# An attention block with an FFN gate on one core: sums over x's quarters taken by token and turned on TensorE, the gate's product spread over the next block, statistics and a square root moved in the prologue

## The chip, the cores and the metric

The kernel runs on one core of a Trainium2 chip, in one launch. The metric is the device time of the launch in microseconds (us). The kernel before took 1982.35 us as the median of three runs (1981.34 to 1983.27).

The engines are named as in the profile: PE is TensorE (PEld its weight loads), DVE is VectorE, ACT is ScalarE, POOL is GpSimd, and SP is the engine from whose queue nearly all DMAs are issued. In the timeline every engine's instructions stand in the order in which the program lists them.

## The reference

The input x has 8 sequences of 256 tokens with 512 features, all in float32. It is normalized, and goes through an attention with 128 heads (latent and rotary parts, head size 4 + 64) and through an FFN whose output, after a SiLU, gates the attention's output:

```python
xn = _layernorm(x, axis=-1)
s = _L0_attn_ref(xn, ...)                    # 128 heads
def _qlora_linear(x, wq, A, B):
    w = jnp.tile(wq, (1, 4))                 # the weight is one quarter, repeated four times
    return x @ w.T + (x @ A.T @ B.T) * 0.5
gate = silu(_qlora_linear(xn, w1q, a1, b1)); up = _qlora_linear(xn, w3q, a3, b3)
g = silu(_qlora_linear(gate * up, w2q, a2, b2))   # hidden size 1376
return x + s * g
```

As each FFN weight is a quarter repeated four times, x @ w.T is the sum of x's four quarters (128 features each) times the quarter. The kernel forms that sum, called xs here, once per block of tokens, and does the same for the hidden layer (function fold).

## The kernel before, in words

**Two phases.** The first phase (function first_phase) computes the layernorm, the FFN's gate and the narrow projections, for the 2048 tokens in four blocks of 512 (index tb, 0 to 3), each of four tiles of 128 tokens (index n). The second phase does attention, block after block of heads; it starts with the score matmuls of L828, and the changed lines do not touch it.

**No scheduler.** The order of the work on each engine is the order in which the Python code writes it. The tile framework only places buffers and adds the waits. PSUM's eight banks of 128x512 float32 come from one pool (function bank). Other buffers rotate by tag: gate and gs and hT have two each, x tiles (xt) six.

**The prologue.** DMAs are issued on SP for x's first block, then the weights, then the six small rows of the LoRA factors (chunk_rows), then x's second block. PE runs 26 transposes of the identity (warm), and four matmuls that spread a weight row over all partitions (first, L627), whose results ACT copies (L635); then two more warm transposes. Function norm takes the statistics with DVE (BN stats and aggregate, L416 and L417, two instructions a tile), and forms 1/sqrt(variance + eps): a bit trick (L428, L430) and three Newton steps, for block 0 on DVE (L436 to L438) and for the other blocks on POOL (L440 to L443, then L449 and L450). Function norm_one applies it, for block 0 on DVE (L459), for others on ACT (L457). Function turn transposes x's tiles on PE (xpt, 16 transposes, L467) and copies them to SBUF as act, features on partitions.

**xs.** Function sums adds the four feature chunks of act: DVE L479, POOL L480 at the same time, DVE L481, and ACT copies the result (L482). xs exists twice, as its row 0 is replaced by a different LoRA row in each (L505). Functions less_first and rest_less_first take the replaced row's weights out of w1 and w3 (L643 on DVE, L655 on POOL).

**One block.** For tb the code calls main(tb, u) for u = 0 to 5. Each but the last makes two pairs of products px and py from xs and w1, w3 (four 128x512 results), then DVE adds the LoRA term (L541 into gate, L545 into hT or in place), ACT takes SiLU of gate (L544), and the product gate * up goes to POOL (L558) or DVE (L556, and L551 and L552 at u = 4 and 5). At u = 3 and 5 fold (POOL, L570 to L572) and low_out (pm2, L582) follow. The next block's x is prepared alongside: norm_one at the u given in the code, and turn at u = 4. After u = 5 come, in this order, sums, narrow (pm and the DVE operation mid, L497, whose rows go to DRAM and come back broadcast as low), low_out(tb, 2) with three DVE operations L594, down (pp, and POOL's differences of x, L158, written to DRAM), gate_out (pf, 48 matmuls, then SiLU into gs, L608, and a DMA to gates_d), and the statistics of block tb + 2. After block 0 POOL lays out weights for the attention (set_up, L744 to L756). In block 3 the first four Project units of the attention are computed among u = 2 to 5.

**Names of places.** on_columns (L173) issues the four matmuls that make one 128x512 result. load_x(tb + 2) is issued on SP at u = 1 and has to wait, for two of its tiles, until turn(tb + 1) has read the buffers.

Of the kernel before, what the change touches and what calls it, by code (L numbers as in the profile page):

```python
# [37 lines left out]
def mla_ffn_gate_kernel(  # L38
# [275 lines left out]
    def first_phase(between):  # L314
# [16 lines left out]
        def load_x(tb):  # L331
            xts[tb] = []
            for n in range(4):
                t = f1.tile([P, D], F32, tag="xt", name=f"xt_{tb}_{n}", bufs=6)
                nc.sync.dma_start(out=t, in_=x[ds(tb * TB + n * P, P), :])
                xts[tb].append(t)
# [22 lines left out]
        for k, wt in enumerate((w1t, w3t)):  # L359
            nc.scalar.dma_start(out=rows[65 + 32 * k : 66 + 32 * k], in_=wt[0:1, :])  # L360
        chunk_rows = f2.tile([P, TB], F32, tag="gs", name="chunk_rows")[:, 0:P]
# [29 lines left out]
        for w_sb, wt in ((w1_sb, w1t), (w3_sb, w3t)):  # L391
            load_chunks(nc.sync, w_sb, wt)

# [13 lines left out]
        load_x(1)  # L407
# [11 lines left out]
        def norm(tb):  # L419


            for n in range(4):
                norm_part(tb, n)
# [3 lines left out]
            i0 = f2.tile([P, 4], I32, tag="i0", name=f"i0_{tb}")  # L427
            nc.vector.tensor_single_scalar(i0, ve.bitcast(I32), 1, ALU.logical_shift_right)  # L428
            r0 = f2.tile([P, 4], I32, tag="r0", name=f"r0_{tb}")
            nc.vector.tensor_scalar(r0, i0, -1.0, float(0x5F3759DF), ALU.mult, ALU.add)  # L430
            r = r0.bitcast(F32)
            e = f2.tile([P, 4], F32, tag="e", name=f"e_{tb}")
            for step in range(3):
# [26 lines left out]

        def turn(tb):
# [12 lines left out]
        def sums(tb):  # L474

            a = xnT[tb]
            xs = [f1.tile([P, TB], F32, tag=f"xs{k}", name=f"xs{k}_{tb}") for k in range(2)]
            xs2 = f1.tile([P, TB], F32, tag="tmp", name=f"xs2_{tb}")
            nc.vector.tensor_add(xs[0], a[:, 0, :], a[:, 1, :])  # L479
            nc.gpsimd.tensor_add(xs2, a[:, 2, :], a[:, 3, :])  # L480
            nc.vector.tensor_add(xs[0], xs[0], xs2)  # L481
            nc.scalar.copy(xs[1], xs[0])  # L482
            xsum[tb] = xs
# [10 lines left out]
        def narrow(tb):  # L494
# [6 lines left out]
            for k in range(2):  # L501
                t = f1.tile([P, TB], F32, tag=f"low{k}", name=f"low{k}_{tb}")
                nc.sync.dma_start(out=t, in_=low_d[tb][k : k + 1, :].to_broadcast([P, TB]))
                lows[tb].append(t)
                nc.scalar.copy(xsum[tb][k][0:1], mid[32 * k : 32 * k + 1])  # L505
# [92 lines left out]
        def gate_out(tb):  # L598
            pfs = [bank(f"pf_{tb}_{n}") for n in range(4)]
            for ks in ((0, 1), (2,)):  # L600
                for n in range(4):
# [4 lines left out]
            for n in range(4):  # L606
# [24 lines left out]

        for i in range(2):
            for k in range(2):
                ps = bank(f"first_{k}_{i}").rearrange("p (q m) -> p q m", q=2)
                nc.scalar.copy(*spread_first(k, ps, *parts[k][i]))  # L635
        warm(2)
# [20 lines left out]
        stats = norm(0)  # L657
# [3 lines left out]
        sums(0)  # L661
        less_first(0, nc.gpsimd)
        narrow(0)
        less_first(1, nc.vector)
        between(-1)
# [7 lines left out]
        rest_less_first(1)  # L673
        for tb in range(NTB):
            more = tb + 1 < NTB
            for u in range(6):
                pj = None
# [10 lines left out]
                if u == 1 and tb == 0:  # L688
                    stats = norm(1)
                if more:  # L690
                    for n in range(4):
                        if u == (n if tb else 2 + n // 2):
                            norm_one(tb + 1, n, *stats)
                if u == 4 and more:
                    turn(tb + 1)
                if u == 1 and tb + 2 < NTB:
                    load_x(tb + 2)
# [6 lines left out]
            if more:  # L704
                sums(tb + 1)
# [5 lines left out]
            gate_out(tb)  # L711
            if tb == 0:
                between(0)
            if tb + 2 < NTB:
                stats = norm(tb + 2)
# [416 lines left out]
```

## Time and profile before

| what | value |
|---|---|
| median of three runs | 1982.35 us |
| the profiled execution's own time | 1983.69 us |
| its span, first to last instruction | 1981.9 us |
| mean granted TensorE clock | 0.998 |
| PE busy | 1964.4 us (99%) |
| DVE, ACT, POOL busy | 1575.9, 1098.0, 758.3 us |
| PE busy from 0 to 218.58 us (first phase) | 206.84 us |

The span is what the trace covers. Times within it count from its start. A timeline row gives an instruction's start and length, the engine, the line, the operation, its output and inputs, and in brackets the idle time of that engine before it and what ended that idle time. PEclk is the share of the full TensorE clock that was granted. An instruction's own length is a little more than the step from one to the next of its kind, since they overlap.

### The profile page before, as it was taken

To read this page: it belongs to the slowest core of one execution; us is meant where nothing else is said; L and a number is where in the kernel's file an instruction comes from. 1 tells how busy PE (TensorE), PEld (TensorE's weight loads), DVE (VectorE), ACT (ScalarE), POOL (GpSimd) and SP (SyncE) were. 2 spreads that over 40 slices of the span, in tenths; PEclk is the share of its full clock that TensorE was granted. 3 is DMA by queue.
4 is the path that set the end of the run, shared out by engine and by line. 5 is a ranking of instruction groups with operands and counts; after the bars stand their busy time and mean duration, and the time that the engine had idled before them with its cause. 6 is when DMAs were issued, how large, how long until landed. Compare 5 with 4: busy or idle time off the path is not lost.

```text
span 1981.9 us, 78697 instructions
## 1 busy us (share of the span) xinstructions
PE 1964.4 (99%) x34033; PEld 1309.7 (66%) x34033; DVE 1575.9 (80%) x2666; ACT 1098.0 (55%) x3029; POOL 758.3 (38%) x1113
## 2 busy tenths in 40 slices
PE   8999999999999999999999999999999999999998
PEld 4334567767777766667776766667776767676775
DVE  7764678888787877788787878788787878888888
ACT  3333465566556555566556555566556555655654
POOL 5877445544552323332332323322332323233232
PEclk9999999999999999999999999999999999999999
DMA  6235322222232223322232322321232222122212
GB/s 195 100 118 179 114 87 87 77 77 87 75 125 89 100 87 101 100 85 68 87 103 89 99 87 101 100 84 69 87 104 88 99 87 86 67 87 87 72 50 87
DMA packets 120017, 187.02 MB, mean 94 GB/s; under 512 B 10715, under 2 KB 84843, under 8 KB 119673
## 3 DMA queue, kind: packets, MB, share of 16 engines
q1 hardware_dynamic: 119665, 181.97, 27.3%
q8 instruction: 270, 4.42, 0.9%
q14 instruction: 74, 0.61, 0.1%
q10 hardware_dynamic: 8, 0.02, 0.0%
HBM read 147.86 MB, written 34.10 MB: 92 GB/s over the span
## 4 chain that ended last, share of the span: by engine, by line
PE 93%; POOL 2%; DVE 2%; issue 1%; DMA 1%; ACT 0%; SPq 0%; POOLq 0%; ACTq 0%; DVEq 0%
PE q L173 40%; PE sc L828 35%; PE av L879 11%; PE po L173 2%; PE pf L173 1%; PE py L173 1%; PE qq L249 1%; PE px L173 1%; POOL h4b L571 0%; POOL hT L558 0%; DVE ring L854 0%; POOL h L570 0%; PE pm L173 0%; DMA xt<-in_x_dram 0%; PE pp L173 0%
## 5 line engine op out<-in xcount | busy, mean ns | idle before, releaser
L847 ACT ACTIVATE pr<-sc,nmx 128x256 f32<-128x256 f32 x2048 | 814.6, 500 | 463.3 <-DVE nmx L841 459.1
L841 DVE TENSOR_REDUCE nmx<-sc 128x2 f32<-128x512 f32 x1024 | 635.5, 683 | 281.7 <-PE sc L828 257.4
L854 DVE STREAM_TRANSPOSE ring<-pr 128x512 f32<-128x512 f32 x1024 | 635.0, 678 | 0.0
L216 POOL TENSOR_TENSOR e<-e,e 128x256 f32<-128x256 f32 x128 | 93.8, 733 | 1042.5 <-ACT e L211 558.8
L173 PE MATMUL q<-x,ws 128*32 128x256 f32 x8192 | 489.0, 379 | 0.7 <-POOL ws L137 0.7
L828 PE MATMUL sc<-act,qr 32*128 32x256 f32 x8192 | 488.3, 374 | 0.0
L828 PEld LDWEIGHTS sc<-act,qr 32*128 32x128 f32 x8192 | 420.7, 185 | 21.8
L173 PEld LDWEIGHTS q<-x,ws 128*32 128x32 f32 x8192 | 266.6, 110 | 176.3 <-POOL ws L137 1.1
L173 PE MATMUL q<-x,w 128*32 128x256 f32 x6144 | 381.7, 381 | 0.9 <-DVE py L545 0.8
L173 PEld LDWEIGHTS q<-x,w 128*32 128x32 f32 x6144 | 187.4, 110 | 155.6 <-ACT pr L847 35.6
L828 PE MATMUL sc<-kc,qcm 32*128 32x256 f32 x4096 | 280.7, 387 | 0.0
L828 PEld LDWEIGHTS sc<-kc,qcm 32*128 32x128 f32 x4096 | 198.0, 184 | 65.0 <-issue 50.4
L879 PE MATMUL av<-ring,vpad 128*32 128x256 f32 (+1 forms) x4160 | 233.4, 376 | 0.1
L211 ACT COPY e<-q 128x256 f32<-128x256 f32 x512 | 202.4, 396 | 26.5 <-PE q L173 26.5
L900 ACT ACTIVATE acc<-av,sides_sb 128x128 f32<-128x128 f32 (+1 forms) x172 | 60.5, 420 | 244.6 <-PE av L879 244.6
L879 PEld LDWEIGHTS av<-ring,vpad 128*32 128x32 f32 x4160 | 134.6, 110 | 88.3 <-issue 1.6
L269 POOL TENSOR_TENSOR qcm<-qc,mask_sb 128x1024 f32<-128x1024 f32 x64 | 122.2, 1910 | 0.0
L217 POOL TENSOR_TENSOR e<-e,e 128x256 f32<-128x256 f32 x128 | 93.6, 731 | 10.0
L218 POOL TENSOR_TENSOR qr<-e,e 128x256 f32<-128x256 f32 x128 | 93.5, 731 | 10.0
L310 POOL COPY vpad<-vall 32x128 f32<-32x128 f32 x256 | 75.4, 294 | 10.2 <-PE av L879 2.3
L228 DVE TENSOR_TENSOR qr<-e,q 128x256 f32<-128x256 f32 x128 | 53.9, 421 | 23.0 <-POOL e L216 17.5
L541 DVE SCALAR_TENSOR_TENSOR gate<-low,bcol_sb,px 128x512 f32<-128x512 f32 x44 | 32.8, 745 | 45.0 <-POOL hT L558 25.7
(124 smaller groups left out, 1138.0 us busy)
## 6 DMA issues: line engine op xcount, KB each, us to landing
w<-in_w_rope_dram SPq DMA_DIRECT2D x128, 512.0 KB
ws<-sums_d SPq DMA_DIRECT2D x96, 512.0 KB
sums_d<-ws SPq DMA_DIRECT2D x32, 512.0 KB
x<-xs_d SPq DMA_DIRECT2D x28, 256.0 KB
xt<-in_x_dram SPq DMA_DIRECT2D x16, 256.0 KB
xs_d<-xt SPq DMA_DIRECT2D x16, 256.0 KB
gate_d<-gs SPq DMA_DIRECT2D x16, 256.0 KB
g<-gate_d SPq DMA_DIRECT2D x16, 256.0 KB
```

The source lines that it names most:

```text
L173: nc.tensor.matmul(to[tile_], w[:, tile_], x, start=start, stop=stop, skip_group_check=True)
L211: nc.scalar.copy(self.e[i], self.banks[i])
L216: nc.gpsimd.tensor_add(m6, m6, m1)
L217: nc.gpsimd.tensor_add(m7, m7, m6)
L218: nc.gpsimd.tensor_add(self.out(1, 1), self.split(m7), self.split(m5))
L269: nc.gpsimd.tensor_mul(qcm, qks[b, sg // 2][0].rearrange("p (q i) -> p q i", i=32).unsqueeze(2).to_broadcast([P, 8, 4, 32]), mask_sb[:, ds ...
L310: nc.gpsimd.tensor_copy(vpad[rows, :, :, 8 * t + 4 * (sg % 2) :][..., :4], valls[b][rows, :, sg])
L828: nc.tensor.matmul(sc[r][:, h, :], lhs.rearrange("p t i -> p (t i)"), rhs, start=(part == 0 and h == 0), stop=(part == 2), skip_group_chec ...
L841: nc.vector.tensor_reduce(nmx[:, r, :], scs[n, f][r], AX.X, ALU.max, negate=True)
L847: nc.scalar.activation(p[:, h, :], scs[n, f][r][:, h, :], AF.Exp, bias=nmxs[n, f][:, r, h : h + 1])
L854: nc.vector.transpose(rings[r][:, (2 * n + f // 2) % 3].rearrange("p k q i -> p q k i")[:, ds(2 * (f % 2), 2)], prs.pop((n, f, r)).rearran ...
L879: nc.tensor.matmul(av[32 * r : 32 * r + 32, cols], vpad[:, k, r, :], rings[r][:, of, k].rearrange("p h q i -> p h (q i)"), start=(k == 0), ...
```

## The change

xs: for the blocks 1 to 3, the function sums no longer adds chunks of the turned x. DVE reduces each normalized x tile over its four quarters, token by token (new function add_quarters, one reduction of 128x512 to 128x128 per tile; its input is read with a step of 128 elements), four more PE transposes (xst) turn the result into a PSUM bank, and ACT copies that bank twice. sums is now called at u = 4, right behind turn. Block 0 keeps the old way.

The gate's product: gate_out(tb) is no longer called whole after block tb, except for the last block. In block tb + 1, each of u = 0 to 3 starts with one of its four tiles.

The statistics: block 1's are taken in pieces in the prologue, with its Newton steps ahead of block 0's first step; those of block tb + 1 for later blocks are taken at u = 0 of block tb, not at the end of block tb - 1. norm_one moves to u = 0 to 3 in block 0, and to u = 1, 2, 3, 3 in others.

The square root: block 0 takes it with ACT, then DVE's reciprocal and a single Newton step in place of the bit trick and three. A first square root of a constant is placed ahead on ACT. The two warm transposes are gone. Block 1's first two x tiles are loaded ahead of the chunk_rows.

```diff
@@ -328,12 +328,11 @@
         f2 = pool("f2", 2, st)
         xts, xns, xnT, xsum, lows = {}, {}, {}, {}, {}
 
-        def load_x(tb):
-            xts[tb] = []
-            for n in range(4):
+        def load_x(tb, tiles=range(4)):
+            for n in tiles:
                 t = f1.tile([P, D], F32, tag="xt", name=f"xt_{tb}_{n}", bufs=6)
                 nc.sync.dma_start(out=t, in_=x[ds(tb * TB + n * P, P), :])
-                xts[tb].append(t)
+                xts.setdefault(tb, []).append(t)
 
         def by_chunks(to, of):
 
@@ -358,6 +357,10 @@
         nc.scalar.dma_start(out=rows[64:97:32], in_=b13[0:33:32, :])
         for k, wt in enumerate((w1t, w3t)):
             nc.scalar.dma_start(out=rows[65 + 32 * k : 66 + 32 * k], in_=wt[0:1, :])
+
+        one = f2.tile([P, 1], F32, tag="sq", name="one")
+        nc.gpsimd.memset(one, 1.0)
+        nc.scalar.activation(one, one, AF.Sqrt)
         chunk_rows = f2.tile([P, TB], F32, tag="gs", name="chunk_rows")[:, 0:P]
         nc.gpsimd.memset(chunk_rows[0:32], 0.0)
 
@@ -390,6 +393,7 @@
         nc.sync.dma_start(out=wdn_sb, in_=w_down.rearrange("(c p) m -> p c m", p=P))
         for w_sb, wt in ((w1_sb, w1t), (w3_sb, w3t)):
             load_chunks(nc.sync, w_sb, wt)
+        load_x(1, range(2))
 
         of = b13[1:34:32, :].rearrange("k (q f) -> q k f", q=4)
         for n in range(2):
@@ -404,7 +408,7 @@
                 out=chunk_rows[16 + 2 * m : 18 + 2 * m, 96 : 96 + w],
                 in_=of[3, :, ds(256 + 32 * m, w)],
             )
-        load_x(1)
+        load_x(1, range(2, 4))
 
         mvs = {}
 
@@ -419,18 +423,25 @@
         def norm(tb):
 
 
-            for n in range(4):
-                norm_part(tb, n)
+            if tb != 1:
+                for n in range(4):
+                    norm_part(tb, n)
             mv = mvs[tb]
             ve = f2.tile([P, 4], F32, tag="ve", name=f"ve_{tb}")
             nc.vector.tensor_scalar_add(ve, mv[:, :, 1], EPS)
-            i0 = f2.tile([P, 4], I32, tag="i0", name=f"i0_{tb}")
-            nc.vector.tensor_single_scalar(i0, ve.bitcast(I32), 1, ALU.logical_shift_right)
-            r0 = f2.tile([P, 4], I32, tag="r0", name=f"r0_{tb}")
-            nc.vector.tensor_scalar(r0, i0, -1.0, float(0x5F3759DF), ALU.mult, ALU.add)
-            r = r0.bitcast(F32)
             e = f2.tile([P, 4], F32, tag="e", name=f"e_{tb}")
-            for step in range(3):
+            if tb:
+                i0 = f2.tile([P, 4], I32, tag="i0", name=f"i0_{tb}")
+                nc.vector.tensor_single_scalar(i0, ve.bitcast(I32), 1, ALU.logical_shift_right)
+                r0 = f2.tile([P, 4], I32, tag="r0", name=f"r0_{tb}")
+                nc.vector.tensor_scalar(r0, i0, -1.0, float(0x5F3759DF), ALU.mult, ALU.add)
+                r = r0.bitcast(F32)
+            else:
+                sq = f2.tile([P, 4], F32, tag="i0", name="sq")
+                nc.scalar.activation(sq, ve, AF.Sqrt)
+                r = f2.tile([P, 4], F32, tag="r0", name="r_first")
+                nc.vector.reciprocal(r, sq)
+            for step in range(3 if tb else 1):
                 new = f2.tile([P, 4], F32, tag=f"r{step}", name=f"r_{tb}_{step}")
                 if tb == 0:
                     nc.vector.scalar_tensor_tensor(e, r, -0.5, r, ALU.mult, ALU.mult)
@@ -457,6 +468,15 @@
                 nc.scalar.activation(xn, xn, AF.Identity, bias=off[:, n : n + 1], scale=one)
             else:
                 nc.vector.tensor_scalar(xn, xn, mv[:, n, 0:1], one, ALU.subtract, ALU.mult)
+
+        quarters = {}
+
+        def add_quarters(tb, n):
+            if n == 0:
+                quarters[tb] = f1.tile([P, 4, P], F32, tag="quarters", name=f"quarters_{tb}")
+            nc.vector.tensor_reduce(
+                quarters[tb][:, n], xns[tb][n].rearrange("p (c s) -> p s c", c=4), AX.X, ALU.add
+            )
 
         def turn(tb):
             a = f1.tile([P, KT, TB], F32, tag="act1", name=f"act1_{tb}")
@@ -475,12 +495,20 @@
 
             a = xnT[tb]
             xs = [f1.tile([P, TB], F32, tag=f"xs{k}", name=f"xs{k}_{tb}") for k in range(2)]
+            xsum[tb] = xs
+            if tb:
+                pt = bank(f"xst_{tb}")
+                for n in range(4):
+                    nc.tensor.transpose(pt[:, ds(n * P, P)], quarters[tb][:, n], ident)
+                for k in range(2):
+                    nc.scalar.copy(xs[k], pt)
+                return
             xs2 = f1.tile([P, TB], F32, tag="tmp", name=f"xs2_{tb}")
             nc.vector.tensor_add(xs[0], a[:, 0, :], a[:, 1, :])
+            norm_part(1, 0)
             nc.gpsimd.tensor_add(xs2, a[:, 2, :], a[:, 3, :])
             nc.vector.tensor_add(xs[0], xs[0], xs2)
             nc.scalar.copy(xs[1], xs[0])
-            xsum[tb] = xs
 
         def over_xn(tb, name, weights):
             ps = bank(f"{name}_{tb}")
@@ -502,6 +530,7 @@
                 t = f1.tile([P, TB], F32, tag=f"low{k}", name=f"low{k}_{tb}")
                 nc.sync.dma_start(out=t, in_=low_d[tb][k : k + 1, :].to_broadcast([P, TB]))
                 lows[tb].append(t)
+            for k in range(2):
                 nc.scalar.copy(xsum[tb][k][0:1], mid[32 * k : 32 * k + 1])
             for j in range(4):
                 nc.sync.dma_start(
@@ -595,15 +624,15 @@
                         to, m2[32 * q : 32 * q + 32], 0.5, to, ALU.mult, ALU.add
                     )
 
-        def gate_out(tb):
-            pfs = [bank(f"pf_{tb}_{n}") for n in range(4)]
+        def gate_out(tb, tiles):
+            pfs = {n: bank(f"pf_{tb}_{n}") for n in tiles}
             for ks in ((0, 1), (2,)):
-                for n in range(4):
+                for n in tiles:
                     for k in ks:
                         on_columns(
                             pfs[n], h4s[tb][:, k, ds(n * P, P)], w2_sb[:, k, :], k == 0, k == 2
                         )
-            for n in range(4):
+            for n in tiles:
                 gs = f2.tile([P, D], F32, tag="gs", name=f"gs_{tb}_{n}")
                 nc.scalar.activation(gs, pfs[n], AF.Silu)
                 nc.sync.dma_start(out=gates_d[4 * tb + n], in_=gs)
@@ -629,11 +658,15 @@
             )
             return one, ps
 
+        copies = []
         for i in range(2):
             for k in range(2):
                 ps = bank(f"first_{k}_{i}").rearrange("p (q m) -> p q m", q=2)
-                nc.scalar.copy(*spread_first(k, ps, *parts[k][i]))
-        warm(2)
+                copies.append(spread_first(k, ps, *parts[k][i]))
+        nc.scalar.copy(*copies[0])
+        stats = norm(0)
+        for copy in copies[1:]:
+            nc.scalar.copy(*copy)
 
         def less_first(k, engine):
             w_sb = (w1_sb, w3_sb)[k]
@@ -654,14 +687,16 @@
                 one = w_sb[:, 8:11][:, a, b]
                 nc.gpsimd.tensor_sub(one, one, firsts[k][:, 8:11][:, a, b])
 
-        stats = norm(0)
         for n in range(4):
             norm_one(0, n, *stats)
         turn(0)
         sums(0)
+        norm_part(1, 1)
         less_first(0, nc.gpsimd)
         narrow(0)
         less_first(1, nc.vector)
+        norm_part(1, 2)
+        norm_part(1, 3)
         between(-1)
         for to, of in ((a2_sb, a2), (w2_sb, w2t), (w2_sb[96:98, 2, :], b2[0:2, :])):
             nc.sync.dma_start(out=to, in_=of)
@@ -671,9 +706,12 @@
         nc.scalar.copy(bcol_sb.rearrange("p c k -> p (c k)"), ps)
         rest_less_first(0)
         rest_less_first(1)
+        stats = norm(1)
         for tb in range(NTB):
             more = tb + 1 < NTB
             for u in range(6):
+                if tb and u < 4:
+                    gate_out(tb - 1, [u])
                 pj = None
                 if not more and u >= 2:
                     pj = Project(u - 2)
@@ -685,14 +723,18 @@
                 if u in (3, 5):
                     fold(tb, u // 2 - 1)
                     low_out(tb, u // 2 - 1)
-                if u == 1 and tb == 0:
-                    stats = norm(1)
                 if more:
                     for n in range(4):
-                        if u == (n if tb else 2 + n // 2):
+                        if u == (min(n + 1, 3) if tb else n) + 1:
+                            add_quarters(tb + 1, n)
+                    if u == 0 and tb:
+                        stats = norm(tb + 1)
+                    for n in range(4):
+                        if u == (min(n + 1, 3) if tb else n):
                             norm_one(tb + 1, n, *stats)
                 if u == 4 and more:
                     turn(tb + 1)
+                    sums(tb + 1)
                 if u == 1 and tb + 2 < NTB:
                     load_x(tb + 2)
                 if tb == NTB - 2 and u == 1:
@@ -702,17 +744,14 @@
                 if not more:
                     between(u + 2)
             if more:
-                sums(tb + 1)
                 narrow(tb + 1)
                 low_out(tb, 2)
                 down(tb + 1)
             else:
                 low_out(tb, 2)
-            gate_out(tb)
+                gate_out(tb, range(4))
             if tb == 0:
                 between(0)
-            if tb + 2 < NTB:
-                stats = norm(tb + 2)
 
         nc.scalar.activation(cks_sb, cks_sb, AF.Exp)
         between(8)
```

## The prediction

> **What bounds the kernel now.** The page first: PE is busy for 1964.4 of 1981.9 us, and the chain of waits is PE for 93%. All edits lie ahead of the first score matmul (L828, 218.51 us); what follows does the same work from there, so I ask only by how much that moment moves. I read PE's busy time and granted clock by stretches, cut where each block's `pp` ends (columns: length, PE busy and instructions, clock, DMA share, GB/s):
>
> ```profile
> 8.00:9.00 1.00, 1.00 (x6) 0.75 1.09 330
> 9.00:15.00 6.00, 5.59 (x24) 0.50 0.58 141
> ...
> 41.90:43.60 1.70, 0.04 (x4) 1.00 0.28 106
> 24.00:59.18 35.18, 31.19 (x316) 1.00 0.45 148
> 59.18:102.65 43.47, 41.90 (x412) 1.00 0.33 113
> 102.65:145.68 43.03, 41.37 (x412) 1.00 0.41 136
> 145.68:218.51 72.83, 70.18 (x1001) 1.00 0.41 141
> ```
>
> PE idles 4.0, 1.6, 1.7 and 2.65 us: this is all that reordering can win. What those waits are, PE's list says:
>
> ```profile
> PE py L173 <- ACT gs L608: 2.3, 2, 1.4
> PE py L173 <- DVE gate L541: 1.7, 1, 1.7
> PE px L173 <- DVE gate L541: 1.6, 3, 0.6
> ...
> PE q L173 <- DVE py L545: 0.8, 1, 0.8
> PE xpt L467 <- DVE hT L556: 0.8, 1, 0.8
> PE pm L582 <- DVE gate L541: 0.8, 1, 0.8
> ```
>
> Behind them stand ACT waiting to reuse a `gs` buffer, and DVE waiting for POOL (timeline):
>
> ```profile
> 162.68 1.22 ACT L608 ACTIVATE gs<-pf 128x512 f32<-128x512 f32 x2 [7.29 <-DMA gate_d<-gs]
> ```
> ```profile
> 42.76 0.75 DVE L541 SCALAR_TENSOR_TENSOR gate<-low,bcol_sb,px 128x512 f32<-128x512 f32 x1 [2.60 <-POOL hT L558]
> ```
>
> The place that decides is the turn at u=4. PE passes it now without the sums:
>
> ```profile
> 88.88 2.30 PE L467 MATMUL xpt<-ident,xt 128*128 128x128 f32 x16
> 91.78 1.07 PE L173 MATMUL px<-xs,w_sb 128*32 128x512 f32 x8 [0.60 <-DVE gate L541]
> ```
>
> while DVE is still at u=4's products until 95.1 and forms the sums much later, at 98.12 and 102.98:
>
> ```profile
> 98.12 1.10 DVE L479 TENSOR_TENSOR xs<-act 128x512 f32<-128x512 f32 x1
> 102.98 1.75 DVE L481 TENSOR_TENSOR xs<-xs,xs 128x512 f32<-128x512 f32 x1 [3.76 <-POOL xs L480]
> ```
>
> There the sums are hidden under 10.5 us of `pf` matmuls. After the change PE itself must wait for DVE's last quarter before px5.
>
> **Steps used.** PE: four matmuls to 512 columns 0.86 (px 113.22, py 114.08); 16 turns 1.97 (132.49), so four 0.5; 32 `pm` or 16 `pp` 3.43. DVE step to step: L541/L545 0.66, L551/L552 and L556 0.71, a BN pair 0.80, a small operation 0.20. POOL: 1.27 a product, 0.28 a small one. The quarter reduction is not in the trace. Lower bound: L841, the same operation on 512 elements read in order, 635.5/1024 = 0.62. Upper bound: L479, a 128x512 DVE operation held back by POOL, 1.10. Its input is strided; of rows that differ by this, POOL L136 (strided halves) takes 0.85 and L216 (in order) 0.73, 1.16 times; L841's mean of 683 ns times that is 0.79. I take 0.8: its own operation with a penalty of that kind. Eight to ten of the twelve quarters stand in PE's wait, so 0.1 more or less of each moves the sum by about 1.
>
> [...]
>
> **Prologue.** *Removed*: two of three Newton steps, the bit trick (about 8 x 0.20), and two warm matmuls (0.69, in PE's gap before 11.03). *Added*: an ACT square root (0.20, as L717), a reciprocal (0.20) and two handovers (0.1 each); the order of instructions shows no more table loads than before. DVE's ve ends at 8.16; root 8.26 to 8.5, reciprocal and one Newton step to 9.3, against 10.43 for L459. ACT does the root between copies for which it waits 0.61 anyway, so these cost nothing. PE's `first` ends at 9.94 and the turn starts there, 1.1 earlier, but at clock 0.50 until 15.15, so 0.5 is won: px at 23.0, not 23.52. Should POOL or ACT be late with the root, up to 1.1 returns; a clock released earlier would win at most 1.7. The two x loads put ahead of the six b13 loads on SP cost those 0.9 (two issues of 0.45); bcol waits for them only at about 21.5 (issued by 15.5), so nothing. The statistics of block 1 go before and after `mid` (gaps of 1.17 and 0.58 in DVE, two parts of 0.8) and after L643 (now ending at 22.75): there two parts and three small operations make 2.2, so the first gate starts at 24.95, not 24.73: that cover is too short, and eats the 0.5.
>
> **Block 0 (to 59.18).** Gone are 3.75 us of statistics on DVE at 33.64. But POOL starts the Newton steps of block 1 only after L655 (about 29.05): 14 x 0.28 reach 33.0, and norm_one(1,0) now stands in ACT's queue ahead of u=1's SiLU. ACT stops there (SiLU was at 30.64); norm_one (0.80) to 33.85, two SiLUs (0.6) to 35.0, DVE's second product to 35.9: u=1 ends there, against 33.64. Then quarter, u=2, quarter, u=3, quarter: 36.7, 39.35, 40.15, 43.5, 44.3; u=4 (four steps of 0.66, four of 0.71) 49.8, last quarter 50.6. PE has had `xpt` since about 45 and waits some 4 us. The last transpose and px5, py5, pm2, pm, pm2, pp (10.3 by the steps) give 61.15 against 59.18: **+2.0**.
>
> **Blocks 1 and 2.** From pf's start: four times 2.57 + 3.43, pm2 0.86, main(4) 3.43, turn 1.94 put PE at 30.25. ACT's `gs` needs one bank per u and a buffer two steps (12 us) old; the wait of 7.29 goes. SP: gate_d of u=2, 3 is queued behind x loads that wait for the turn; nobody needs these buffers until the next block. Statistics at u=0 (3.75 on DVE against 2.6 of spare time beside pf) delay u=1 by 1.1; caught up by u=2 (3.4 of DVE in 6.0 of PE). In block 1 set_up (7.7 on POOL, 64.80) now lies ahead of products instead of under pf; DVE is 2.8 late at u=2, level by u=3, PE covered by banks: nothing, up to +1. At u=3 DVE's product waits for py of 24.02 and ends at 25.5, quarter 26.3. At u=4 py's end (28.31) bounds: 28.35 + 0.66 + 4 x 0.71 = 31.85, two quarters 33.45, transpose 33.7. **PE waits 3.0 us**. Plus 10.3: 44.0; I add 0.3 for small gaps. Against the mean of 43.47 and 43.03: +1.05 each, **+2.1**. Without the xs chain, `mid` and L594 finish 1 to 4 us before PE needs them.
>
> **Block 3.** Its pf work moves between u=0 and 3; no quarters. The waits of 1.39 (gs) and 0.81 go; x loads no longer wait for four gs. Rows left over: 0.2 before the last pf, some 0.4 at banks: of 2.65 about 2.0 is won (between 0 and 2.65): **-2.0**.
>
> **Sum**: 2.0 + 2.1 - 2.0 = +2.1 on a profiled execution of 1983.69 (span 1981.9), which lies 1.34 above the median; so 1982.35 + 2.1 = **1984.5**. A difference under 0.2% (4.0 us) is what a measurement of this kernel cannot tell from none.
>
> **Rivals.**
> 1. *The quarters are dear*: at 1.10 each, block 0 has four and the other two have three after u=3's product: 10 x 0.3 = +3.0: 1987.5. For: strided input. [...] It passes 0.2% from 1.0 up.
> 2. *The clock falls in the waits*: it stood at 0.50 for 6.7 us from about 8.5 although PE was at work; in 41.90:43.60, almost idle, it stayed 1.00. My waits are 3 to 4 us. One fall of 3.4 to 6.7 us at half speed costs 1.7 to 3.3: one gives 1986 to 1988, three up to 1994.5. [...]
> 3. *No wait at the sums (faster)*: DVE reaches the quarters as PE finishes the turn. Without the waits of 4 in block 0 and 3.0 twice, +2.1 becomes -7.9: 1974.5. It decides once 6.1 of these 10 are gone. For: PE may itself be late through banks. Against: py's end and five to six DVE steps stand in order behind it.
>
> **How the numbers follow.** My forecast 0.45; dear quarters 0.18; clock 0.20; no wait 0.13; other 0.04. The forecast's own range, quarter 0.62 to 0.95 (+0.7 to +3.6) and block 3 from 0 to -2.65 (+2.0 to -0.65 on top), is 1982.4 to 1988. The whole range, without the outer parts of rivals 2 and 3, is 1979 to 1990.5. Faster by over 0.2%: 0.13 (rival 3). Slower: dear quarters and clock 0.38, less what falls short, plus my own upper end: 0.37. Within: 0.50.
>
> **What would show it.** After: L477 between 0.62 and 1.1; PE idle 3 us ahead of `xst` or the px behind it, released by DVE, in each of three blocks; clock 1.00 behind these; no `gs` wait for DMA; ACT idle before norm_one(1,0) until about 33; pp's of blocks 0 to 2 ending near 61, 105.5 and 150, scores starting near 220.6. I am wrong if the wait is not there, if the clock drops, or if a POOL, bank or SP wait appears that I called covered.

## The result and the profile after

The changed kernel takes 1994.21 us (median of 5 runs, 1993.6 to 1995.2), the kernel before 1981.94 us beside it: a ratio of 1.0062, with a 95% interval of 1.0051 to 1.0073. It is slower by 12 us, where the prediction said 2 and allowed 8.

The profiled execution of the changed kernel has a span of 1993.0 us. First PE by stretches, cut again where each block's `pp` ends and the scores start (columns: length, busy time and instructions of PE, PEld, DVE, ACT and POOL, PE's clock, DMA share, GB/s):

```profile
9.00:15.00 6.00, 6.00 (x22) 3.82 (x18) 2.93 (x7) 2.81 (x5) 1.32 (x7) 0.52 0.90 242
24.00:64.89 40.89, 33.54 (x320) 11.45 (x316) 31.43 (x48) 16.04 (x28) 28.15 (x41) 0.92 0.41 132
64.89:111.44 46.55, 43.26 (x417) 14.69 (x412) 33.09 (x51) 17.43 (x29) 35.50 (x70) 0.96 0.32 109
111.44:159.10 47.66, 44.52 (x416) 15.11 (x412) 31.47 (x50) 17.55 (x29) 27.59 (x35) 0.93 0.38 122
159.10:230.00 70.90, 69.83 (x1000) 28.99 (x992) 27.81 (x42) 21.90 (x45) 48.39 (x57) 1.00 0.43 143
```

Block 0 ends 5.7 us later than before (64.89 against 59.18). Blocks 1 and 2 take 3.1 and 4.6 more (46.55 and 47.66 against 43.47 and 43.03). The last block takes 1.9 less. The scores start 11.5 us later, so the whole loss lies in three blocks. There PE idles more, and its clock is no longer 1.00. PE's list of waits says where it idles (total, times, longest):

```profile
PE xst L502 <- DVE quarters L477: 10.3, 5, 3.9
PE xpt L487 <- DVE gate L570: 1.0, 1, 1.0
...
PE q L173 <- issue: 0.8, 1, 0.8
```

The waits behind ACT's `gs` are gone; in their place stands one new wait, in five parts, for DVE's quarters. PE's timeline at the turn of block 2 (start, length, what, idle time before and its releaser):

```profile
144.54 0.47 PE L502 MATMUL xst<-ident,quarters 128*128 128x128 f32 x1 [2.67 <-DVE quarters L477]
145.49 0.48 PE L502 MATMUL xst<-ident,quarters 128*128 128x128 f32 x1 [0.47 <-DVE quarters L477]
145.89 1.93 PE L173 MATMUL px<-xs,w_sb 128*32 128x512 f32 x8
147.60 1.93 PE L173 MATMUL py<-xs,w_sb 128*32 128x512 f32 x8
149.31 1.93 PE L611 MATMUL pm<-hT,a_sb 128*32 128x512 f32 x8
```

The reader sees the wait, and then what the prediction did not have: from one start to the next px, py and pm2 take 1.71 us instead of 0.86. PE is working, at half its clock. The windows of 2 us behind the waits in blocks 0 and 2 show it:

```profile
52.00:54.00 2.00, 1.36 (x9) 0.49 (x13) 0.58 (x1) 0.00 (x0) 1.86 (x3) 0.50 0.00 0
54.00:56.00 2.00, 2.00 (x16) 0.49 (x12) 0.75 (x1) 0.59 (x1) 0.18 (x1) 0.56 0.00 0
56.00:58.00 2.00, 2.00 (x32) 0.84 (x28) 1.22 (x2) 1.11 (x2) 0.00 (x0) 1.00 0.00 0
146.00:148.00 2.00, 2.00 (x12) 0.48 (x16) 0.11 (x1) 0.11 (x1) 0.00 (x0) 0.50 0.00 0
148.00:150.00 2.00, 2.00 (x12) 0.39 (x8) 0.94 (x2) 0.85 (x2) 0.00 (x0) 0.50 0.00 0
```

Taking px, py, pm2 and the last transposes at their steps here less their steps at full clock gives 1.5, 1.7 and 2.8 us for the three falls, 6.0 in all. In block 0 the clock fell already at 48.93, 0.2 us into the wait of 3.88, and stayed down until 55.75. DVE's groups give the price of a quarter, 1.02 to 1.10 us (nanoseconds, min/median/max):

```profile
L477 DVE TENSOR_REDUCE quarters<-xt x12: 1022/1065/1098, 37.1 to 144.4; 128x128 f32<-128x512 f32 x12
```

### The profile page after: what moved, and what is told of

The parts are those of the page before. It is cut to its first block, busy times and chain, and to the rows that moved or that the text cites. A ratio compares the mean times of both kernels' runs of the same rounds, so it can differ in the third digit from the quotient of the medians.

```text
span 1993.0 us, 78715 instructions
## 1 busy us (share of the span) xinstructions
PE 1970.5 (99%) x34043; PEld 1311.4 (66%) x34043; DVE 1582.4 (79%) x2665; ACT 1100.0 (55%) x3034; POOL 753.7 (38%) x1111
## 4 chain that ended last, share of the span: by engine, by line
PE 94%; DVE 2%; DMA 2%; POOL 1%; issue 1%; ACT 0%; SPq 0%; DVEq 0%; POOLq 0%; ACTq 0%
PE q L173 39%; PE sc L867 34%; PE av L918 11%; PE po L173 2%; PE pf L173 2%; PE py L173 1%; PE px L173 1%; PE qq L249 1%; DMA wo_sb<-in_w_o_dram 1%; PE pm L173 1%; PE pp L173 1%; DVE ring L893 0%; PE pm L611 0%; PE vps L294 0%; DVE py L574 0%
## 5 line engine op out<-in xcount | busy, mean ns | idle before, releaser
L310 POOL COPY vpad<-vall 32x128 f32<-32x128 f32 x256 | 75.4, 294 | 10.2 <-PE av L918 2.3
L570 DVE SCALAR_TENSOR_TENSOR gate<-low,bcol_sb,px 128x512 f32<-128x512 f32 x44 | 32.7, 744 | 47.8 <-PE px L173 43.9
```

The lines of the kernel that those rows point to most:

```text
L310: nc.gpsimd.tensor_copy(vpad[rows, :, :, 8 * t + 4 * (sg % 2) :][..., :4], valls[b][rows, :, sg])
```

## The experiments

The theory after the result: the loss is PE's wait at xst (place and price of the quarters) plus the clock that falls behind it. The rivals: that the spread of the gate's product or the prologue costs the time; that the clock costs nothing where DVE is late anyway; that the wait only moves when the sums move.

**Keeping PE at work in the wait** (e1_keep_warm).

```
+ for _ in range({1: (0, 0, 2, 15)}.get(tb, (0, 0, 10, 1))[n]):
+     nc.tensor.transpose(pt[:, ds(n * P, P)], ident, ident)
  nc.tensor.transpose(pt[:, ds(n * P, P)], quarters[tb][:, n], ident)
```

> Edit: while PE waits for the last quarters (3.9 us in block 0, 2.7 and about 0.6 in blocks 1 and 2) it transposes the identity, 17 times in block 0 and 11 times in the others, into columns that the real transposes overwrite. Theory T (the wait stays, and the granted clock of 0.50 to 0.73 behind each wait costs about 1.5 + 1.7 + 2.8 = 5.9 us): the clock stays 1.00 behind xst, px, py and pm2 are back at 0.86 a step, 1988.3 us (1987.3 to 1990). Rival R (the clock in these stretches costs nothing, since DVE is late there anyway): 1993.5 to 1995.

Measured: 1989.80 us (1988.44 to 1993.53), ratio to before 1.0042 (1.0028 to 1.0055): 4.4 less than the changed kernel. An idle transpose took 0.12, less than I had reckoned, so gaps of 1.6 to 2.0 us were left, and still the clock stood at 1.00 in all three blocks of the profiled execution:

```profile
61.70:106.54 44.84, 42.75 (x427) 16.06 (x423) 33.12 (x51) 17.44 (x29) 34.64 (x69) 1.00 0.34 113
106.54:151.40 44.86, 42.76 (x428) 16.02 (x423) 31.50 (x50) 17.56 (x29) 27.50 (x35) 1.00 0.41 130
```

Blocks 1 and 2 fell by 1.7 and 2.8, the two sizes reckoned from the slowed steps. Block 0 ended 3.2 earlier, but 1.7 of that is an earlier start (its first px at 21.86 against 23.60; in the prologue of this execution the clock was at 0.50 for 3.4 us, in that of the changed kernel for 6.8), which leaves the 1.5 reckoned. The clock is a real part of the loss, by these steps 6.0 of 11.5 us and by the medians 4.4 of 12, and the rival that it costs nothing falls. The repair is not certain: of the five runs, those with 1991.85 and 1993.53 us had a mean granted clock of 0.997 and 0.996, the three others 0.999. The wait itself remained.

**The sums issued later** (e2_sums_later): same quarters, same transposes, behind the `pm` matmuls.

```
   turn(tb + 1)
-  sums(tb + 1)
...
-  nc.vector.tensor_scalar_mul(mid, over_xn(tb, "pm", ck_sb), cks_sb[:, 0:1])
+  ps = over_xn(tb, "pm", ck_sb)
+  if tb:
+      sums(tb)
+  nc.vector.tensor_scalar_mul(mid, ps, cks_sb[:, 0:1])
```

> Edit: the same quarters and the same four transposes, but issued behind the pm matmuls of the next block's narrow step, instead of ahead of the last px. Theory T (PE stands at xst because DVE is still at u=4's products): PE has px, py, pm2 and pm (4.3 us) to do in between, so the waits at xst (4.5, 3.3, 3.1 us) shrink to under 1.5 each and the clock stays 1.00; 1994.2 - 10.9 - 5.9 and up to 4 for smaller waits at pm2: 1978 to 1982. Rival R (the wait only moves: DVE's backlog of quarters holds h, and PE waits as long at pm2, with the same clock): 1991 to 1995.

Measured: 1977.96 us (10 runs), ratio 0.9979 (0.9970 to 0.9988): 16.2 less than the changed kernel, and faster than the kernel before. Windows and PE's timeline at the turn of block 0:

```profile
60.09:101.90 41.81, 41.81 (x420) 17.81 (x415) 31.34 (x51) 17.44 (x29) 34.73 (x69) 1.00 0.35 116
101.90:143.51 41.61, 41.61 (x417) 15.41 (x409) 31.49 (x50) 17.45 (x29) 27.57 (x35) 1.00 0.42 141
```
```profile
51.09 3.64 PE L173 MATMUL pm<-act,ck_sb 128*32 128x256 f32 x64
54.66 0.66 PE L502 MATMUL xst<-ident,quarters 128*128 128x128 f32 x4
55.24 1.42 PE L614 MATMUL pm<-hT,a_sb 88*32 88x512 f32 x8
```

In blocks 1 and 2 PE is busy for the whole of the stretch. The wait did not move to pm2: DVE finishes its quarters (the last one of block 0 at 52.60) while PE does px, py, pm2 and pm (48.15 to 54.66; these steps add up to 6.0 us, not to the 4.3 of my expectation). So the place of four transposes is worth 16 us, wait and clock together.

**The spread and the sums, each with the other undone** (e3_old_sums, e4_gate_at_end, e8_later_gate_end). The first forms the sums as before, at the end of the block, and keeps the spread:

```
-  add_quarters(tb + 1, n)
-  sums(tb + 1)          # at u == 4
+  sums(tb + 1)          # ahead of narrow(tb + 1), by chunk adds
```

> Edit: the sums of x formed as before (two adds on DVE and one on POOL over the turned x, at the end of the block); no quarters and no xst; all the rest of the change stays (gate's product spread over the next block, square root, statistics ahead). Theory T (the loss lies in the quarters and their place; the rest of the change is a small gain): no waits at xst, no xst (0.25 each, 12 of them), but a wait of up to 2 us per block before the first px, since only one pf now lies between pp and px and the copy of mid's row ended 4.5 us after pp's start of the next step in the kernel before; 1978 to 1983. Rival R (the spread of the gate's product is what costs): 1988 to 1994.

The second keeps the changed kernel's sums and puts the gate's product back; the third does the same to the kernel with the later sums:

```
-  if tb and u < 4:
-      gate_out(tb - 1, [u])
...
   else:
       low_out(tb, 2)
-      gate_out(tb, range(4))
+  gate_out(tb, range(4))     # in every block, at its end
```

> Edit: the gate's product whole at the end of its block, as before; quarters, xst, square root and statistics stay as in the changed kernel. Theory T (the spread of the gate's product gains the waits for gs, 1.9 us in the last block, and gives DVE slack in u=0 to 3): 1996 to 1999, with the same or longer waits at xst and the same clock of 0.5 behind them. Rival R (the spread is what costs): below 1990.

> Edit: sums issued later (the run with 1978.0), but the gate's product whole at the end of its block, as before. It prices the spread of the gate's product where the sums no longer stop PE. Theory T (the spread fills PE while DVE does the statistics, normalized tiles and quarters, and takes away the waits for gs, 2 us in the last block): 1981 to 1986. Rival R (the spread is worth nothing once the sums are later): 1977 to 1979.5.

Measured medians beside each other (the kernel before, 1982.3 to 1982.6 in these comparisons, has another prologue and other places for the statistics as well):

| sums of x | gate's product at the block's end | spread over the next block |
|---|---|---|
| chunk adds, end of the block | 1982 (before) | 1992.2 (ratio 1.0047, 1.0035 to 1.0060) |
| quarters, ahead of the last px | 2003.1 (1.0104, 1.0090 to 1.0117) | 1994.2 (after) |
| quarters, behind pm | 1988.9 (1.0032, 1.0020 to 1.0044) | 1978.0 (0.9979, 0.9970 to 0.9988) |

The spread gains 9 to 11 us with the quarters, much more than the 2 I had given it, and loses 10 with the old sums. My expectation for the first of the three (1978 to 1983) was wrong. Its timeline (PE, then DVE) shows why:

```profile
62.24 1.93 PE L173 MATMUL pf<-w_sb,h 128*32 128x512 f32 x8 [5.53 <-issue]
```
```profile
55.48 1.75 DVE L504 TENSOR_TENSOR xs<-xs,xs 128x512 f32<-128x512 f32 x1 [3.76 <-POOL xs L503]
57.26 0.75 DVE L519 TENSOR_SCALAR mid<-pm,cks_sb 128x512 f32<-128x512 f32 x1
60.00 2.14 DVE L617 SCALAR_TENSOR_TENSOR h<-pm,h 32x512 f32<-32x512 f32 x3 [1.99 <-ACT h L615]
```

The last third of `pf` needs the rows that DVE folds at L617 (done at 62.14; PE's line calls its wait "issue"), and these are queued on DVE behind the sums, which wait for POOL. With four tiles of `pf` in a row that end was needed 7 us after the start of `pf`; with one tile it is needed after 1.7, and PE stops for 5.5 us here and for 3.75 in each of the next two blocks, with the clock falling again (0.93 in the block behind the first stop). So the quarters do serve the spread.

Where the gate's product stands at the end, two windows of the later-sums kernel show what is lost (DVE's busy time is the third busy figure), against the same kernel with the spread:

```profile
90.00:94.00 4.00, 2.30 (x16) 0.99 (x16) 4.00 (x6) 2.22 (x4) 3.92 (x4) 1.00 0.46 127
108.00:114.00 6.00, 6.00 (x63) 3.23 (x59) 0.00 (x0) 0.32 (x1) 1.23 (x1) 1.00 0.90 323
```
```profile
86.00:90.00 4.00, 4.00 (x36) 2.30 (x29) 4.00 (x6) 2.17 (x4) 3.92 (x4) 1.00 0.00 0
```

While PE is at `pf`, DVE has nothing at all to do for 6 us (108 to 114). At the turn (90 to 94) DVE is busy without a gap and PE idles 1.7 of 4 us. Spread out, the `pf` work lies beside DVE's work, and the same turn (86 to 90) runs without idling.

**The price of a quarter** (e5_two_adds, e9_in_order). First by adds that read in order:

```
- nc.vector.tensor_reduce(quarters[tb][:, n], xn.rearrange("p (c s) -> p s c", c=4), AX.X, ALU.add)
+ nc.vector.tensor_add(q[:, n : n + 2], xn[:, 0:2], xn[:, 2:4])      # n < 3; the last by three adds
+ nc.vector.tensor_add(q[:, n], q[:, n], q[:, n + 1])
```

> Edit: the changed kernel with its sums in their place, but each quarter formed by adds that read in order (256 columns, then 128; the last quarter by three adds of 128) instead of one reduction with a strided read (1.02 a step). Estimate from 0.66 a step for 512 columns and 0.20 for a small operation: 0.6 a quarter. Theory T (the prices of the quarters stand in PE's wait, and the clock falls only behind the longer waits: 2.67 us made it fall, 2.04 us with idle transposes ahead did not): ten quarters by 0.4 = 4 us less waiting, and the clock stays up in blocks 1 and 2: 1985 to 1988.5. Rival R (the wait is set by u=4's products, not by the quarters): 1992 to 1995.

Measured: 1998.21 us, ratio 1.0080 (1.0068 to 1.0093). Both expectations fail: it is slower by 4. The groups of quarters:

```profile
L479 DVE TENSOR_TENSOR quarters<-xt x9: 418/477/931, 36.4 to 149.3; 128x256 f32<-128x256 f32 x9
L480 DVE TENSOR_TENSOR quarters<-quarters x9: 293/1257/1295, 36.8 to 149.8; 128x128 f32<-128x128 f32 x9
```

An add of 128 columns takes 0.29 at best and 1.26 in the median. The eight long ones all stand beside POOL's products for `hT` or its adds of `h` (about 1.3 each): at 45.76 an add of 128 columns lasts 1.23 to 46.99, and POOL's L605 runs from 45.38 to 46.85. All twelve reductions of the changed kernel, which read one input, lie between 1.02 and 1.10: 1.08 at 37.06, where POOL is idle, and 1.10 at 40.69, beside its products.

So the price had to be asked with the reduction itself, by its order of reading alone (it then adds neighbouring columns, which are not the sums that the kernel needs):

```
- xns[tb][n].rearrange("p (c s) -> p s c", c=4)
+ xns[tb][n].rearrange("p (s c) -> p s c", c=4)
```

> Edit: the changed kernel, but the reduction sums four neighbouring columns instead of the four quarters, so it reads its 512 elements in order. It leaves out the right sums (xs holds other sums of x), the instructions are the same in number, shape and place. Theory T (the hop from quarter to quarter is the price: 1.02 a step against 0.62 for the row of scores' maxima that reads in order): 0.6 to 0.7 a quarter, ten of them in PE's wait, 4 us less waiting, the clock stays 1.00 in blocks 1 and 2: 1985 to 1989. Rival R (a reduction of groups of four costs as much in order): 1.0 to 1.1 a quarter, 1993.5 to 1995.

Measured: 1987.57 us (7 runs), ratio 1.0028 (1.0018 to 1.0039), 6.6 less than the changed kernel. The group of quarters, and PE at the turn of block 1:

```profile
L477 DVE TENSOR_REDUCE quarters<-xt x12: 675/680/686, 36.6 to 139.7; 128x128 f32<-128x512 f32 x12
```
```profile
95.79 0.33 PE L502 MATMUL xst<-ident,quarters 128*128 128x128 f32 x1 [2.20 <-DVE quarters L477]
96.39 0.33 PE L502 MATMUL xst<-ident,quarters 128*128 128x128 f32 x1 [0.26 <-DVE quarters L477]
96.65 1.06 PE L173 MATMUL px<-xs,w_sb 128*32 128x512 f32 x8
97.53 1.04 PE L173 MATMUL py<-xs,w_sb 128*32 128x512 f32 x8
```

In order a reduction takes 0.68, with the hop 1.07: the hop is a factor of 1.57, not the 1.16 I took. The waits shorten by 0.8 and 0.7 in blocks 1 and 2, and in this execution the clock stood at 1.00 behind them (in block 0 it still fell), which gives more than the shorter waits themselves: from `pf` to `pf` these two blocks take 44.0 us each, against 46.5 and 47.7.

**When the clock falls** (e11_less_warm): the first experiment with 10, 3 and 1 idle transposes in blocks 0, 1 and 2.

```
- {1: (0, 0, 2, 15)}.get(tb, (0, 0, 10, 1))[n]
+ {1: (0, 0, 0, 10), 2: (0, 0, 3, 0), 3: (0, 0, 1, 0)}[tb][n]
```

> Edit: as the run with idle transposes, but fewer of them (10, 3 and 1 in blocks 0, 1 and 2, at 0.12 us each), so that PE's gap ahead of the last or third quarter is about 2.6, 2.3 and 2.5 us. Without them gaps of 2.67 brought the clock to 0.50, with more of them gaps of 2.04 and 1.58 did not. Theory T (the clock falls by the length of one gap): it falls in some of the three, the longest first, none below 2.04; 1989.5 to 1994. Rival R (it falls by how busy PE was over a longer stretch, which a few transposes hardly change): it falls in all three as in the changed kernel, 1993 to 1995.

Measured: 1991.36 us (2 runs), profiled span 1990.9. The turns of blocks 1 and 2:

```profile
94.19 0.33 PE L504 MATMUL xst<-ident,quarters 128*128 128x128 f32 x1 [2.35 <-DVE quarters L477]
95.14 0.33 PE L504 MATMUL xst<-ident,quarters 128*128 128x128 f32 x1 [0.61 <-DVE quarters L477]
95.40 1.10 PE L173 MATMUL px<-xs,w_sb 128*32 128x512 f32 x8
96.28 1.92 PE L173 MATMUL py<-xs,w_sb 128*32 128x512 f32 x8
...
140.74 0.47 PE L504 MATMUL xst<-ident,quarters 128*128 128x128 f32 x1 [2.56 <-DVE quarters L477]
141.68 0.47 PE L504 MATMUL xst<-ident,quarters 128*128 128x128 f32 x1 [0.47 <-DVE quarters L477]
142.08 1.94 PE L173 MATMUL px<-xs,w_sb 128*32 128x512 f32 x8
```

In block 1 the clock fell behind 2.35 and 0.61, late, at py, for 3.4 us; in block 2 behind 2.56 and 0.47, before px, for 6.8. In block 0 the gap ahead of the last quarter came out at 1.52 and px behind it ran at full speed, but the clock had fallen there too: from 45.10 to 48.51 it stood at 0.50, behind gaps of 0.78 and 0.99 us, and the ten idle transposes took 0.22 each instead of 0.12. So it fell in all three blocks, and theory T, by which one gap's length decides and none below 2.04 counts, fails, although the time lies in its range.

What decides can be read from the moments at which the clock changes. In one execution they lie on a grid: in the changed kernel at 48.93, 55.75, 100.13, 103.54, 144.50 and 151.33, all of them whole numbers of 3.413 us apart (51.20 us from the first to the third are 15 such steps). The same holds in the trace of every run, each with its own offset, and up to the end of the span every stretch at half clock lasted 3.4 or 6.8 us, once 10.2. These are pairs of neighbouring steps of the grid, cut in block 0 of the changed kernel, of this run, and of the run with more idle transposes (length and PE's busy time first, PE's clock third from the end):

```profile
45.51:48.93 3.42, 1.66 (x11) 0.97 (x10) 3.42 (x6) 1.32 (x3) 3.34 (x4) 1.00 0.41 149
48.93:52.34 3.41, 0.00 (x0) 0.00 (x0) 3.32 (x5) 1.88 (x4) 3.27 (x4) 0.50 0.00 0
```
```profile
41.68:45.10 3.42, 1.66 (x14) 1.15 (x11) 3.32 (x6) 1.68 (x3) 3.34 (x4) 1.00 0.45 153
45.10:48.51 3.41, 2.83 (x15) 2.63 (x13) 3.33 (x7) 2.61 (x6) 3.41 (x3) 0.50 0.02 5
```
```profile
47.04:50.45 3.41, 1.83 (x17) 1.59 (x15) 3.32 (x6) 2.03 (x5) 3.33 (x3) 1.00 0.00 0
50.45:53.87 3.42, 2.97 (x29) 1.05 (x33) 1.76 (x3) 1.28 (x3) 1.88 (x3) 1.00 0.00 0
```

Between 24 and 230 us the fourteen traces have 808 steps at full clock. Behind each of the 14 in which PE was busy for 1.41 us or less the clock fell; behind the ten with 1.42 to 1.80 it fell six times; behind the 784 with 1.82 or more it never did. So in these traces a step of which PE idled about half or more put the clock at risk, in one gap or in several, and a given wait may fall into one step or be split between two: over the same gaps of 0.78, 0.99 and 0.60 us in block 0 the clock fell in the two executions above (in the changed kernel 0.2 us into the wait that follows) and not in those of e1_keep_warm and e2_sums_later. Rival R is nearer with its longer stretch, but that stretch is one step, and a few transposes do change it. This is read from the traces afterwards; no run was made to test it. It does not hold in the prologue, where the clock fell behind steps with 2.2 us and more of PE's busy time (2.48 in the changed kernel, 3.30 in the kernel before).

**The prologue and block 0** (e6_later_norm, e7_later_two, e10_norm_alone, e12_no_root). Block 0 forms the statistics of block 1 after its first pair and normalizes one step later, on top of the later sums:

```
- stats = norm(1)                                   # ahead of the loop
- if u == 0 and tb:
+ if u == 0:
      stats = norm(tb + 1)
- if u == (min(n + 1, 3) if tb else n):
+ if u == min(n + 1, 3):                            # norm_one; the quarter one step behind
```

> Edit: sums issued later as in the run of that name (1978.0), and block 0 forms the statistics of block 1 after its first pair of products, and normalizes its tiles one step later, as the other blocks do. Theory T (block 0's remaining 3.3 us of PE waits come from DVE's start at 27.7 instead of 25 and from ACT, which stands for POOL's Newton steps ahead of the second pair's SiLU): first gate near 25.3, 1.5 to 2.5 us less: 1975.5 to 1976.7. Rival R (the delay moves to the last quarters, which now all lie in u=2 to 4): 1977.5 to 1979.5.

Measured: 1975.92 us, ratio 0.9965 (0.9953 to 0.9978). The first gate starts at 23.91 instead of 27.73, and block 0's `pp` ends at 56.4 instead of 60.1. Of these 3.7 us, 1.6 are from an earlier start in that one execution (px at 22.27 against 23.87; in its prologue the clock was at 0.50 for 3.4 us instead of 6.8); the medians differ by 2.0, as the theory said. DVE's three small operations there take 0.25, 0.17 and 0.17, and ACT's wait for POOL's steps is 1.3 instead of 4.0. This is the fastest version, 0.35% below the kernel before. On top of it, the quarters by adds, and the square root undone (shift, constant, three Newton steps and the two idle transposes again):

> Edit: the run before with the quarters by adds read in order. Theory T: PE has no wait at xst left in blocks 1 and 2, so cheaper quarters help block 0 alone, by up to 1 us: 1974.5 to 1976.7. Rival R (DVE is the bound of the blocks even with the sums later): 4 us less, 1971 to 1973.

> Edit: the run with 1975.9, but the first block's statistics by the shift, the constant and three Newton steps again, behind the copies, and the two idle transposes back: the square root alone undone. Theory T (px of block 0 starts at the same time with and without, 23.60 against 23.52, so the root is worth nothing that a measurement shows): 1975.0 to 1977.0. Rival R (with DVE on the path of block 0 the root is worth its 1 us or more): 1977.0 to 1979.

Measured: 1982.36 (0.9998, 0.9989 to 1.0007) and 1976.05 (0.9967, 0.9956 to 0.9979). The adds cost 6.4, against both expectations: those of 128 columns take up to 1.30 beside POOL's work here too, so that DVE is late for the turn of block 0, and behind a PE gap of 2.15 us there the clock falls too (PE was busy for 1.25 us of the grid's step from 41.34). By the end of that block's `pp` 2.8 of the 6.4 have arisen:

```profile
44.39 0.76 PE L492 MATMUL xpt<-ident,xt 128*128 128x128 f32 x4 [2.15 <-DVE gate L578]
45.62 1.93 PE L173 MATMUL px<-xs,w_sb 128*32 128x512 f32 x8 [0.47 <-DVE gate L578]
```

The square root is worth nothing that can be measured. The later norm on the changed kernel alone:

> Edit: of the run with 1975.9 only the later statistics and normalized tiles in block 0; the sums stay ahead of the last px. Theory T (block 0's late start on DVE, 27.5 against 24.7 before, is part of the 5.7 us that block 0 lost): 1 to 2.5 us less than the changed kernel, 1991.7 to 1993.2. Rival R (the quarters then come last together, and the wait at xst grows by as much): 1993.5 to 1996.

Measured: median 1993.81, ratio 1.0047 (1.0033 to 1.0061), but in two groups: two runs at 1986.4 and 1986.7, four from 1993.2 to 1995.2. The profiled execution is one of the latter: block 0's `pp` ends at 63.95, 0.9 earlier than in the changed kernel, and block 1 loses 1.2 of that again, because its clock stays down longer (6.8 us, not 3.4). So the early norm is some 1 us of block 0's loss there. What the two short runs did was not profiled. Their mean granted clock was 0.996, that of the other four 0.993 or 0.994, and the three falls of the changed kernel cost 6.0 us of its time, near these 8; but a run of the changed kernel with 0.996 took 1993.6, so that the clock is the cause here is argued only.

## Why the prediction was wrong

**The step that failed: the clock behind the waits, put at nothing.** The sum of +2.1 has no term for it, and the list of signs says "clock 1.00 behind these". Measured, the falls cost 1.5, 1.7 and 2.8 us, 6.0 of the 9.4 by which the forecast fell short of the 11.5. I had this case as rival 2, with the right number of falls and the right end ("three up to 1994.5"), and gave all of it a chance of 0.20 and then left its outer part out of the range. What misled me was the row at 41.90, where PE sat almost idle for 1.7 us at clock 1.00; how long a wait makes the clock fall, no row of before showed. The lower of the two lengths in rival 2, 3.4 us, stood in no row of before either; the changed kernel then showed falls of 3.41 us once and 6.83 twice. The clock's grid splits the row at 41.90 between two steps, from 39.21 and from 42.63, in which PE was busy for 2.67 and 2.09 us, and neither is half idle. My own forecast of the waits was 3 to 4 us; a wait of 3 us idles the step that it fills most for 1.5 to 3 us, by where it lies, and so it was not safe. Idle transposes in the waits gave back 4.4 us of the median.

**The quarter was mis-sized, at 0.8 instead of 1.02 to 1.10.** The upper bound (1.10, L479) was the right end, though for another reason: in the kernel before, L479, an add of two inputs, took 1.10 at 98.12, beside POOL's L570 and L571, and 0.69 at 15.55, where POOL's L480 began after it; the reduction took 1.02 to 1.10 beside POOL's work or not, and 0.68 without the hop. The penalty of 1.16 was taken from POOL rows, and DVE's own is 1.57 (1.07 against 0.68). I had priced 0.1 of a quarter at 1 us. In order, 0.39 less was worth 6.6, since with the shorter waits the clock also fell less often.

**Block 0, +2.0 forecast, +5.7 measured.** Three terms. POOL was to start its Newton steps at 29.05; in the profile of before this is about where its second set of L655 begins (29.00), and that set ends at 30.2. It started at 30.58, and u=1's second product ended at 37.1 instead of 35.9: 1.2. Four quarters at 0.2 more: 0.9. So the last quarter ended at 52.58, against 50.6. From there to the end of `pp` it took 12.3 instead of 10.55: 1.75, mostly the clock (1.5). The three small operations, forecast at 0.20 each, took 0.76 and 1.20 beside POOL's differences of x (L158) and 0.34 beside its memset (L685), and DVE came to them 1.0 later than forecast, so the first gate started at 27.48 and not at 24.95; here this is covered by ACT's wait for POOL.

**Blocks 1 and 2, +1.05 each forecast, +3.1 and +4.6 measured.** The waits at xst were said to be 3.0; they are 3.28 and 3.14. That part of the path, DVE's six steps behind py's end and then the quarters, came out as worked. Against the 44.3 worked out for each block 2.25 and 3.36 are missing: the clock's 1.7 and 2.8, and 0.28 and 0.14 of longer waits; 0.3 and 0.4 are left over. The surcharge of up to 1 for set_up did not come.

**What held.** Block 3: -2.0 forecast, -1.93 measured, with no `gs` wait for DMA left in that block. The prologue is net zero, with px at 23.60 against 23.52 before, though not by its terms (px was to come at 23.0, and DVE was to eat that gain); the run without the square root agrees. ACT idle until POOL's steps were done (norm_one at 34.49, forecast 33.05). Rival 1 (dear quarters, 1987.5) was true as far as it went; it and rival 2 came together, which my separate cases did not allow for: the dear quarter lengthens the very wait behind which the clock falls. Rival 3 (no wait, 1974.5) was wrong for the change, but the kernel with the later sums is that case, at 1978.0.

**Where the gain went.** The spread of the gate's product with quarters is worth 9 to 11 us, not the 2 of the `gs` waits: I had counted the waits it removes and not DVE's idling beside 10 us of `pf`. With the sums behind pm the whole change is 4 us faster than before (1978.0); ahead of the last px they cost 16.

## What to carry to other kernels

Before moving work that waits for another engine into PE's order, ask what PE still has to do behind it, and issue the waiting matmuls after that: here the same four transposes cost 16 us ahead of 6 us of ready matmuls and no wait behind them. Price waits that idle PE for about half of a 3.4 us step of its clock's grid or more, one long or several short, with a half-speed stretch of 3.4 or 6.8 us behind them (here behind every step with 1.41 us or less of PE's busy time and six of ten with 1.42 to 1.80; the same gaps met it in two executions and not in two others), and let two doubtful costs that feed the same wait share one case in the range. When a block's one engine idles in one half and is late in the other, spreading PE's independent product over the steps is worth more than the waits it visibly removes.

## What the runs showed of the hardware

- PE's clock changed only at moments that lie whole numbers of 3.413 us apart in one execution, with an offset that differs between executions. From 24 to 230 us it fell to 0.50 behind every such step in which PE was busy for 1.41 us or less, behind six of ten with 1.42 to 1.80, and behind none with 1.82 or more; gaps of 0.78 and 0.99 us were enough once. An offset that differs between executions would let the clock fall in some runs of one kernel and not in others; two groups of runs of one kernel, 8 us apart (e10_norm_alone), fit that but do not show it.
- A DVE add of 128 columns with both inputs in SBUF took 0.29 us at best and 1.23 to 1.39 beside POOL's operations of 512 columns (e5_two_adds). A reduction of 512 elements to 128 took 0.68 in order (e9_in_order) and 1.07 with a hop at each element, and in the changed kernel no more than 1.10 in any of twelve places, beside POOL's work or not.
- Three DVE operations on 4 elements each, 0.17 apiece in the kernel before (from 36.96), took 0.76 and 1.20 in the changed kernel (from 25.32) beside POOL's differences of 512 columns, and 0.34 beside its memset of 384.
